# Own terms moved ahead of the update, and two PSUM banks shared by column, in layer 1 of a four-layer graph network

## The chip, the cores and the metric

One core of one Trainium2 chip runs the whole network in one launch. The metric is the device time of that launch in microseconds (us). Engines are named as the profile names them: PE (TensorE matmul), PEld (its weight loads), DVE (VectorE), ACT (ScalarE), POOL (GpSimd) and SP (SyncE, which here only issues DMAs).

## The reference

N = 2708 nodes have 128 features each; the adjacency matrix has about 0.6% entries that are not zero. Four layers follow one another, each with a residual and a layer norm. The change lies in layer 1, which is, cut to what matters:

```
s = x @ msg_w[:, :D].T                  # own term of each node
d = x @ msg_w[:, D:].T                  # a neighbour's term
messages   = gelu(s[:, None] + d[None, :] + msg_b)
aggregated = einsum('ijd,ij->id', messages, adj)
new = concat([x, aggregated]) @ upd_w.T + upd_b
h   = gelu(new) + x ;  h = layernorm(h) * ln_w + ln_b
x   = layernorm(x + h)
```

Layer 2, `A @ (x @ W) + b`, is partly done beside it.

## The kernel before

The rows are sorted by the number of their neighbours and cut into 22 blocks of up to 128. Layer 1 goes through the blocks in 22 turns, in the order `TURNS`. `CAPS` gives the neighbours of a block's longest row, 30 in the first and 8 in the shortest.

A turn has these parts.

- `own_row` (L854) loads the block's own rows by a DMA of SP into `x_s`: half 0 holds d of the node itself, half 1 holds x. The pool has three buffers. The loop asks for it one turn ahead.
- `messages` (L865) takes a PSUM bank `po` (tile `own`, one buffer). In its first quarter it transposes x (L870); ACT copies that into `x_st` (L871); two matmuls put the own term, with the bias, into the second quarter `s_ps` (L872, L873). DVE adds it to the node's own d (L887), ACT applies Gelu (L888), DVE weighs it (L882). For each chunk of up to 8 neighbours POOL issues one gather per neighbour slot (L247, an indirect DMA into `msg`, five buffers), DVE adds `s_ps` (L896), ACT applies Gelu (L899), and DVE weighs and accumulates each slot (L884) in the first and last quarters of `po`; the last two go to `parts` in SBUF. In turns 3 to 9 and 15 to 19 two `spread` calls follow, which lay out lists for layer 3: DVE multiplies (L618), PE multiplies into the third quarter of `po` (L624), DVE copies out (L631, L632).
- For the later blocks of the adjacency, `transposed` (PE L964, L969 and ACT L974 copies, SP writes L976) and `extract` (DVE, the neighbour lists) are emitted next.
- `update` (L905) takes the PSUM bank `tail` (one buffer). PE transposes and sums the two parts (L910), ACT copies (L917), PE multiplies with the two weights and the bias (L919 to L921), ACT applies Gelu (L926), DVE adds and normalises twice (L927 to L935), POOL scatters the new rows (L936, helper line L255), PE transposes them (L937) and multiplies with layer 2's weight (L941), with ACT copies L939 and L942. `x_b` (L915) is a sum that the first layer norm adds; it has two buffers.
- Further `transposed` calls for the earlier blocks, and from turn 11 on two `layer2` calls a turn (two at most; POOL gathers a row of the transposed adjacency, ACT writes `weighed` in L1007, one buffer, PE does L1014 and L1018).

No order is written out by hand here. A scheduler puts each engine's instructions into one fixed queue at compile time: among those that it takes to be ready, the one that stands earlier in the program goes first. It also derives all semaphores from what the instructions read and write. On the chip each queue runs strictly in its order.

Of the kernel before, what the change touches and what calls it, by code (L numbers as in the profile page):

```python
# [9 lines left out]
FP = mybir.dt.float32  # L10
AF = mybir.ActivationFunctionType
ALU = mybir.AluOpType
# [3 lines left out]
P = 128  # L16
N = 2708
D = 128
NFULL = N // P
NREM = N - NFULL * P  # L20
NBLK = NFULL + 1
# [40 lines left out]
BLOCKS = [(b * P, min(P, N - b * P)) for b in range(NBLK)]  # L62
# [5 lines left out]
TURNS = [*range(19), 21, 19, 20]  # L68
# [17 lines left out]
def gnn_resnorm_kernel(  # L86
# [21 lines left out]
    nc = tc.nc  # L108

    const = ctx.enter_context(tc.tile_pool(name="const", bufs=1))  # L110
    ident = const.tile([P, P], FP, name="ident")
# [127 lines left out]
    ones = keep.tile([P, P], FP, name="ones")  # L239
# [92 lines left out]
    own_ps = graph.enter_context(tc.tile_pool(name="own_ps", bufs=1, space=PSUM))  # L332
# [4 lines left out]
    with ExitStack() as layer:  # L337
# [355 lines left out]
        ws_t = weight(msg_w[:, 0:D], "ws_t")  # L693
# [3 lines left out]
        msgb = row_on_all(work, msg_b, "msgb")  # L697
# [151 lines left out]
        mine = layer.enter_context(tc.tile_pool(name="mine", bufs=2))  # L849
        bank = graph.enter_context(tc.tile_pool(name="bank", bufs=6, space=PSUM))  # L850
        tail_ps = graph.enter_context(tc.tile_pool(name="tail_ps", bufs=1, space=PSUM))
        xw = xs

        def own_row(b):  # L854
            n = BLOCKS[b][1]
            x_s = mine.tile([P, 2, D], FP, name="x_s", bufs=3)
            nc.sync.dma_start(
                x_s[0:n],
                dx_dram[int(b >= SPLIT)][b * P : b * P + n, 0 : 2 * D].rearrange(
                    "p (t d) -> p t d", t=2  # L860
                ),
            )
            return x_s

        def messages(b, x_s, three):  # L865
            n, kk = BLOCKS[b][1], CAPS[b]
            po = own_ps.tile([P, 512], FP, name="own", tag="own")
            x_st, s_ps = mine.tile([P, P], FP, name="x_st"), po[:, P : 2 * P]
            acc = (po[:, 0:P], po[:, 3 * P : 4 * P])
            nc.tensor.transpose(po[:, 0:n], x_s[0:n, 1, :], ident[0:n, 0:n])  # L870
            nc.scalar.copy(x_st[:, 0:n], po[:, 0:n])  # L871
            nc.tensor.matmul(s_ps[0:n], lhsT=x_st[:, 0:n], rhs=ws_t, start=True, stop=False)  # L872
            nc.tensor.matmul(  # L873
                s_ps[0:n], lhsT=ones[0:1, 0:n], rhs=msgb[0:1, :], start=False, stop=True
            )
            parts = mine.tile([P, 2, D], FP, name="parts")
            def weigh(k, m):
                last = acc[k % 2][0:n]
                to = parts[0:n, k % 2, :] if k >= kk - 1 else last
                v = ls[0:n, b, k : k + 1]  # L880
                if k < 2:
                    nc.vector.tensor_scalar(to, m, v, None, ALU.mult)  # L882
                else:
                    nc.vector.scalar_tensor_tensor(to, m, v, last, ALU.mult, ALU.add)  # L884

            mk = x_s[0:n, 0, :]
            nc.vector.tensor_tensor(mk, mk, s_ps[0:n], ALU.add)  # L887
            nc.scalar.activation(mk, mk, AF.Gelu)  # L888
            weigh(0, mk)
            for c0, c1 in chunks_of(kk):  # L890
                kc = c1 - c0
                msg = msgs.tile([P, 8, D], FP, name="msg")
                for k in range(kc):
                    gather(msg[0:n, k, :], d_dram, idx[0:n, b, c0 + k + 1 : c0 + k + 2])
                mk = msg[0:n, 0:kc, :]
                nc.vector.tensor_tensor(  # L896
                    mk, mk, s_ps[0:n].unsqueeze(1).to_broadcast((n, kc, D)), ALU.add
                )
                nc.scalar.activation(mk, mk, AF.Gelu)  # L899
                for k in range(kc):  # L900
                    weigh(c0 + k + 1, msg[0:n, k, :])
            for i, b3 in enumerate(three):
                spread(b3, po, 256 + 64 * i)
            return x_st, parts

        def update(b, x_s, x_st, parts):
            n = BLOCKS[b][1]
            tp = tail_ps.tile([P, 512], FP, name="tail")
            for i in range(2):
                nc.tensor.matmul(  # L910
                    tp[:, 0:n], lhsT=parts[0:n, i, :], rhs=ident[0:n, 0:n],
                    start=(i == 0), stop=(i == 1),
                )
            x_b = mine.tile([P, D], FP, name="x_b")
            nc.vector.tensor_tensor(x_b[0:n], x_s[0:n, 1, :], lnb[0:n], ALU.add)  # L915
            agg_t = mine.tile([P, P], FP, name="agg_t")
            nc.scalar.copy(agg_t[:, 0:n], tp[:, 0:n])  # L917
            pn = tp[0:n, P : 2 * P]
            nc.tensor.matmul(pn, lhsT=x_st[:, 0:n], rhs=u1_t, start=True, stop=False)  # L919
            nc.tensor.matmul(pn, lhsT=ones[0:1, 0:n], rhs=updb[0:1, :], start=False, stop=False)  # L920
            nc.tensor.matmul(pn, lhsT=agg_t[:, 0:n], rhs=u2_t, start=False, stop=True)  # L921
            new = mine.tile([P, 1, D], FP, name="new")
            x_n = mine.tile([P, 1, D], FP, name="x_n")
            sums = mine.tile([P, 2], FP, name="sums1")
            h, s0, s1 = new[0:n, 0, :], sums[0:n, 0:1], sums[0:n, 1:2]
            nc.scalar.activation(h, pn, AF.Gelu)  # L926
            nc.vector.scalar_tensor_tensor(  # L927
                h, h, 1.0, x_s[0:n, 1, :], ALU.mult, ALU.add, accum_out=s0
            )
            rstd = deviation(mine, n, 1, new[0:n], s0)  # L930
            nc.vector.scalar_tensor_tensor(h, h, s0, lnw[0:n], ALU.add, ALU.mult)
            nc.vector.scalar_tensor_tensor(
                h, h, rstd[0:n, 0:1], x_b[0:n], ALU.mult, ALU.add, accum_out=s1
            )
            normalised(mine, n, 1, new[0:n], s1, x_n[0:n])  # L935
            scatter(x2_dram, perm[0:n, b : b + 1], x_n[0:n, 0, :])  # L936
            nc.tensor.transpose(tp[:, 256 : 256 + n], x_n[0:n, 0, :], ident[0:n, 0:n])  # L937
            x_nt = mine.tile([P, P], FP, name="x_nt")
            nc.scalar.copy(x_nt[:, 0:n], tp[:, 256 : 256 + n])  # L939
            px = tp[0:n, 384:512]  # L940
            nc.tensor.matmul(px, lhsT=x_nt[:, 0:n], rhs=w2_l2, start=True, stop=True)  # L941
            nc.scalar.copy(xw[0:n, b, :], px)  # L942

# [86 lines left out]

        rows_of[NFULL] = searched_again(NFULL)
        again = list(range(SPLIT))
        ahead = own_row(0)
        left = list(range(SPLIT, NBLK))
        for i, b in enumerate(TURNS):
            if i == SPLIT - 2:
                sorted_lists(1)
            x_s, ahead = ahead, own_row(TURNS[i + 1]) if i + 1 < NBLK else None
            three = beside3(i)
            if i == 2 or i == SPLIT + 1:  # L1040
                for b3 in beside3(i + 1):
                    load3(b3)
            for b3 in beside3(i + 2) if three or beside3(i + 1) else []:
                load3(b3)
            x_st, agg = messages(b, x_s, three)
            for _ in range(2 if i < 1 else 1):
                if left:
                    e = left.pop(0)
                    with behind():
                        transposed(e, rows_of[e], True)  # L1050
                        run(extract(e, rows_of[e]))
                    if e == NBLK - 3:
                        run(place(SPLIT, NBLK - 2, lists(SPLIT, NBLK - 2)))
                    if e == NBLK - 1:
                        run(place(NBLK - 2, NBLK, lists(NBLK - 2, NBLK)))
            update(b, x_s, x_st, agg)
            if second and i:
                own_scatter(*second.pop(0))
            if i == 2:
                column_sums_of(0)  # L1060
            if i == 10:
                column_sums_of(1)

            for _ in range(2 if i in (9, 10, 11) else 1):
                if i and again:
                    e = again.pop(0)
                    transposed(e, load(e))
            if i == 11:
                accs2.extend(banks("acc2_"))
            if i >= 11:  # L1070
                for k in range(2 * (i - 11), min(i, 2 * (i - 10))):
                    layer2(k)
# [25 lines left out]
    with ExitStack() as layer:  # L1098
# [26 lines left out]
        for b0, count, n in quads():  # L1125
# [5 lines left out]
            for j in range(count):  # L1131
                nc.tensor.matmul(
                    ps_v[:, 0:D], lhsT=ones[0:n, :], rhs=sq[0:n, j, :],
                    start=(b0 + j == 0), stop=(b0 + j == NBLK - 1),
# [48 lines left out]
        for b0, count, n in quads():  # L1183
# [34 lines left out]
            for j in range(count):  # L1218
                at = slice(j * P, j * P + n)
# [19 lines left out]
    with ExitStack() as layer:  # L1239
        work = layer.enter_context(tc.tile_pool(name="s3", bufs=1))  # L1240
        mine = layer.enter_context(tc.tile_pool(name="s3_mine", bufs=2))
# [55 lines left out]
        own, closing, finishing, preparing, wide, sums_of = {}, [], [], [], [], {}  # L1297
# [242 lines left out]
        ahead = repeated(*quads[0], gathered[0])  # L1540
# [556 lines left out]
```

## Time and profile before

| | us |
|---|---|
| median of 3 runs (1930.33 to 1936.26) | 1935.91 |
| the profiled execution's own time | 1938.44 |
| its span, first to last instruction | 1936.7 |
| layer 1's turns, first transpose L870 to the last copy L942 | 204.5 to 1025.8 |

Busy time in that stretch of 821.3 us, from the view of busy time in windows: PE 388.4, PEld 318.6, DVE 380.3, ACT 239.3, POOL 406.9. The granted clock of TensorE is 0.61 of full speed in it, the DMA engines are busy 0.46.

A row of a group or tile view reads: line, engine, operation, out<-in, count, then durations (least, median, greatest, in ns) and first and last start. A row of the timeline reads: start, duration, engine, line, operation, out<-in, shapes, count, and in brackets the engine's idle time before it and what ended it; "remote" is a semaphore whose last update the view can't put to an instruction.

### The profile page before, as it was taken

How to read it: one execution, taken by the hardware profiler on the slowest of the kernel's cores; microseconds unless marked ns; L12 is line 12 of the kernel's file. 1: busy time of each engine (PE TensorE's matmuls, PEld its weight loads, DVE VectorE, ACT ScalarE, POOL GpSimd, SP SyncE). 2: the span in 40 equal slices, each digit the busy share in tenths (PEclk: the TensorE clock that was granted, in tenths of full speed). 3: DMA queues.
4: the chain of work that ended last, by engine and by line, in shares of the span. 5: the costliest groups of instructions: out<-in, count | busy, mean ns of one | idle time of the engine just before them, and what ended most of it. 6: DMA issues, size and time to landing. Idle time of an engine off the chain costs nothing. (4 is left out here: it accounts for less than half of the span.)

```text
span 1936.7 us, 23643 instructions
## 1 busy us (share of the span) xinstructions
PE 1240.9 (64%) x5771; PEld 864.1 (45%) x5771; DVE 1166.6 (60%) x4895; ACT 776.5 (40%) x3156; POOL 892.8 (46%) x1003
## 2 busy tenths in 40 slices
PE   7974313353446553554673748888788788878885
PEld 7973212242334442554663314544444444444444
DVE  8997445675635423433447417777678677676774
ACT  3565345543324210211122415555455555445553
POOL 1004654445653366445331474655555556555430
PEclk9986555555555576776676756676676777666675
DMA  8642645666545525223231574865566655756540
GB/s 283 238 150 79 131 140 165 174 183 174 141 103 142 177 43 160 95 92 140 79 113 44 167 239 131 212 190 163 145 196 183 182 166 160 191 150 192 150 115 7
DMA packets 167676, 289.63 MB, mean 150 GB/s; under 512 B 49600, under 2 KB 121502, under 8 KB 160429
## 3 DMA queue, kind: packets, MB, share of 16 engines
q0 software_dynamic: 60496, 190.77, 34.4%
q1 hardware_dynamic: 99489, 92.57, 15.6%
q10 hardware_dynamic: 7544, 4.69, 1.0%
q8 instruction: 48, 0.79, 0.2%
q14 instruction: 99, 0.81, 0.1%
HBM read 242.51 MB, written 45.36 MB: 149 GB/s over the span
## 5 line engine op out<-in xcount | busy, mean ns | idle before, releaser
L247 POOL DMA_INDIRECT g<-t_dram,idx x400 | 398.6, 996 | 316.0 <-issue 178.9
L247 POOL DMA_INDIRECT msg<-d_dram,idx x368 | 348.6, 947 | 260.2 <-issue 164.8
L1389 ACT ACTIVATE sum_junk<-g 126x128 bf16<-126x128 f32 (+3 forms) x1024 | 301.3, 296 | 142.4 <-issue 59.8
L1358 PE MATMUL z<-x,copies 32*126 32x512 f32 (+3 forms) x800 | 221.3, 944 | 65.8 <-DVE g L1555 45.0
L969 PE MATMUL pt_a<-ident,rows 128*128 128x128 f32 (+2 forms) x475 | 114.1, 395 | 144.4 <-ACT at_sb L974 79.5
L1555 DVE TENSOR_TENSOR g<-g,z 126x1536 f32<-126x1536 f32 (+3 forms) x100 | 175.0, 1750 | 44.0 <-DMA g<-t_dram,idx 15.3
L1018 PE MATMUL acc<-x_nat,at_rows 128*128 128x128 f32 (+2 forms) x968 | 160.7, 326 | 52.3 <-DMA at_rows<-at_dram,perm 26.5
L1389 ACT ACTIVATION_READ_ACCUMULATOR sum_junk<-g 126x1 f32 (+3 forms) x1024 | 191.6, 187 | 0.0
L1018 PEld LDWEIGHTS acc<-x_nat,at_rows 128*128 128x128 f32 (+2 forms) x968 | 144.1, 232 | 65.5 <-issue 38.7
L1363 PE MATMUL z<-g,ident 126*126 126x512 f32 (+3 forms) x200 | 169.3, 941 | 0.7 <-issue 0.7
L1435 PE MATMUL po_s<-wm,g 126*128 126x24 f32 (+6 forms) x800 | 128.6, 316 | 58.5 <-DVE wm L1422 56.2
L1435 PEld LDWEIGHTS po_s<-wm,g 126*128 126x128 f32 (+3 forms) x800 | 124.8, 243 | 75.6 <-DVE wm L1422 67.9
L969 PEld LDWEIGHTS pt_a<-ident,rows 128*128 128x128 f32 (+2 forms) x475 | 82.9, 205 | 167.5 <-ACT at_sb L974 92.8
L884 DVE SCALAR_TENSOR_TENSOR own<-msg,ls,own 128x128 f32<-128x128 f32 (+1 forms) x302 | 105.6, 350 | 85.4 <-ACT msg L899 28.5
L1381 DVE SCALAR_TENSOR_TENSOR g<-g,a_ps 126x1536 f32<-126x1536 f32 (+6 forms) x100 | 151.0, 1510 | 0.0
L420 PE MATMUL acc<-x_nat,rows 128*128 128x129 f32 (+3 forms) x1012 | 128.5, 288 | 26.0 <-DMA rows<-in_adj_dram 14.9
L420 PEld LDWEIGHTS acc<-x_nat,rows 128*128 128x128 f32 (+2 forms) x1012 | 123.0, 198 | 31.2 <-DMA rows<-in_adj_dram 16.0
L1358 PEld LDWEIGHTS z<-x,copies 32*126 32x126 f32 (+3 forms) x800 | 67.8, 261 | 100.3 <-issue 46.5
L899 ACT ACTIVATE msg<-msg 128x896 f32<-128x896 f32 (+4 forms) x55 | 50.4, 917 | 132.9 <-DVE msg L896 92.1
L1373 DVE SCALAR_TENSOR_TENSOR g<-z,a 126x128 f32<-126x128 f32 (+3 forms) x400 | 91.9, 285 | 19.5 <-remote 9.2
L445 DVE FIND_INDEX8 ci<-cv,rows 128x8 uint32<-128x247 f32 (+2 forms) x242 | 98.7, 408 | 0.0
L1363 PEld LDWEIGHTS z<-g,ident 126*126 126x126 f32 (+3 forms) x200 | 42.0, 263 | 124.3 <-issue 117.3
(302 smaller groups left out, 2132.2 us busy)
## 6 DMA issues: line engine op xcount, KB each, us to landing
rows<-in_adj_dram SPq DMA_DIRECT2D x34, 1354.0 KB
at_dram<-at_sb SPq DMA_DIRECT2D x105, 256.0 KB
g<-t_dram,idx POOLq DMA_INDIRECT x400
msg<-d_dram,idx POOLq DMA_INDIRECT x368
t_dram<-t_row SPq DMA_DIRECT2D x21, 256.0 KB
x_s<-dx_dram SPq DMA_DIRECT2D x21, 128.0 KB
at_dram<-at_sb SPq DMA_DIRECT2D x21, 64.0 KB
t_dram<-x_nat SPq DMA_DIRECT2D x5, 256.0 KB
```

The lines of the kernel that those rows point to most:

```text
L247: nc.gpsimd.indirect_dma_start(out=dst, out_offset=None, in_=table[0:N, :], in_offset=bass.IndirectOffsetOnAxis(ap=index, axis=0),)
L420: nc.tensor.matmul(accs0[k][0:m, c0 : c0 + f1 - f0], lhsT=rows[0:n, j0 : j0 + m], rhs=x_nat[0:n, b, f0:f1], start=k not in started, stop=( ...
L445: nc.vector.max_index(out=ci[0:n, at], in_max=cv[0:n, at], in_values=rows[0:n, c0 : c0 + cw])
L884: nc.vector.scalar_tensor_tensor(to, m, v, last, ALU.mult, ALU.add)
L969: nc.tensor.transpose(pt[0:m, j, 0:n], rows[0:n, c0 : c0 + m], ident[0:n, 0:n])
L1018: nc.tensor.matmul(accs2[ib // 4][0:m, (ib % 4) * D : (ib % 4 + 1) * D], lhsT=at[0:n, i0 : i0 + m], rhs=xw[0:n, b, :], start=(k == 0 and i ...
L1358: nc.tensor.matmul(z3[0:e, r, :] if r < 3 else z1[0:e], lhsT=copies[g][rows, j, :], rhs=own[b][1][rows, :], start=True, stop=r < 3, skip_g ...
L1363: nc.tensor.matmul(z1[0:e], lhsT=ident[0:e, 0:e], rhs=g4[0:e, 3, 0:HD], start=False, stop=True, skip_group_check=True,)
L1381: nc.vector.scalar_tensor_tensor(z, z, 0.0, a_ps[0:e].unsqueeze(1).to_broadcast((e, count, HD)), ALU.max, ALU.mult)
L1389: nc.scalar.activation(junk[0:e], g4[0:e, r, hd * D : (hd + 1) * D], AF.Identity, accum_out=sc[0:e, r, hd : hd + 1],)
L1435: nc.tensor.matmul(po[:, p0 * HEADS : (p0 + g) * HEADS], lhsT=g4s[i][0:e, r, HD : HD + D], rhs=wm[0:e, 4 * i + r, :, :], start=True, stop= ...
L1555: nc.vector.tensor_tensor(z, z, z3[0:e], ALU.add)
```

## The change

The own term is computed in a function of its own, `own_terms`, which the loop calls for the next turn's block after this turn's `messages` and `transposed`/`extract` and before this turn's `update`. Its transpose and its two matmuls use the second quarter of a bank `sums1` that is taken once for all turns. A new ACT copy moves the own term from PSUM to an SBUF tile `s` (two buffers), and the two adds of `messages` read `s`. The accumulators and the spreads use the other quarters of `sums1`. `own_row` is asked for two turns ahead. The updates get a bank `updates`, also taken once, of which even turns use the first half and odd turns the second; the last transpose and product use the columns that the first ones used. `x_b` has one buffer.

```diff
+        def own_terms(b, x_s):
+            n = BLOCKS[b][1]
+            x_st = mine.tile([P, P], FP, name="x_st")
+            s = mine.tile([P, D], FP, name="s")
+            at = sums1[:, P : 2 * P]
+            nc.tensor.transpose(at[:, 0:n], x_s[0:n, 1, :], ident[0:n, 0:n])
+            nc.scalar.copy(x_st[:, 0:n], at[:, 0:n])
+            nc.tensor.matmul(at[0:n], lhsT=x_st[:, 0:n], rhs=ws_t, start=True, stop=False)
+            nc.tensor.matmul(at[0:n], lhsT=ones[0:1, 0:n], rhs=msgb[0:1, :], start=False, stop=True)
+            nc.scalar.copy(s[0:n], at[0:n])
+            return x_s, x_st, s
...
-        def messages(b, x_s, three):
+        def messages(b, x_s, s, three):
...
-            po = own_ps.tile([P, 512], FP, name="own", tag="own")
-            x_st, s_ps = mine.tile([P, P], FP, name="x_st"), po[:, P : 2 * P]
-            acc = (po[:, 0:P], po[:, 3 * P : 4 * P])
-            nc.tensor.transpose(po[:, 0:n], x_s[0:n, 1, :], ident[0:n, 0:n])
-            nc.scalar.copy(x_st[:, 0:n], po[:, 0:n])
-            nc.tensor.matmul(s_ps[0:n], lhsT=x_st[:, 0:n], rhs=ws_t, start=True, stop=False)
-            nc.tensor.matmul(
-                s_ps[0:n], lhsT=ones[0:1, 0:n], rhs=msgb[0:1, :], start=False, stop=True
-            )
+            acc = (sums1[:, 0:P], sums1[:, 3 * P : 4 * P])
...
-            nc.vector.tensor_tensor(mk, mk, s_ps[0:n], ALU.add)
+            nc.vector.tensor_tensor(mk, mk, s[0:n], ALU.add)
...
-                    mk, mk, s_ps[0:n].unsqueeze(1).to_broadcast((n, kc, D)), ALU.add
+                    mk, mk, s[0:n].unsqueeze(1).to_broadcast((n, kc, D)), ALU.add
...
-                spread(b3, po, 256 + 64 * i)
-            return x_st, parts
+                spread(b3, sums1, 256 + 64 * i)
+            return parts
...
-        def update(b, x_s, x_st, parts):
+        def update(b, x_s, x_st, parts, tp):
...
-            tp = tail_ps.tile([P, 512], FP, name="tail")
...
-            x_b = mine.tile([P, D], FP, name="x_b")
+            x_b = mine.tile([P, D], FP, name="x_b", bufs=1)
...
-            nc.tensor.transpose(tp[:, 256 : 256 + n], x_n[0:n, 0, :], ident[0:n, 0:n])
+            nc.tensor.transpose(tp[:, 0:n], x_n[0:n, 0, :], ident[0:n, 0:n])
...
-            px = tp[0:n, 384:512]
+            px = tp[0:n, P : 2 * P]
...
-        ahead = own_row(0)
+        sums1 = own_ps.tile([P, 512], FP, name="sums1", tag="own")
+        updates = tail_ps.tile([P, 512], FP, name="updates", tag="tail")
+        rows1 = [own_row(b) for b in TURNS[:2]]
+        terms = [own_terms(TURNS[0], rows1.pop(0))]
...
-            x_s, ahead = ahead, own_row(TURNS[i + 1]) if i + 1 < NBLK else None
+            x_s, x_st, s = terms.pop(0)
+            if i + 2 < NBLK:
+                rows1.append(own_row(TURNS[i + 2]))
...
-            x_st, agg = messages(b, x_s, three)
+            agg = messages(b, x_s, s, three)
...
-            update(b, x_s, x_st, agg)
+            if rows1:
+                terms.append(own_terms(TURNS[i + 1], rows1.pop(0)))
+            update(b, x_s, x_st, agg, updates[:, 256 * (i % 2) : 256 * (i % 2) + 256])
```

More of the change, by code (lines that the diff above doesn't have):

```diff
@@ L936, in update @@
             scatter(x2_dram, perm[0:n, b : b + 1], x_n[0:n, 0, :])
-            nc.tensor.transpose(tp[:, 256 : 256 + n], x_n[0:n, 0, :], ident[0:n, 0:n])
+            nc.tensor.transpose(tp[:, 0:n], x_n[0:n, 0, :], ident[0:n, 0:n])
             x_nt = mine.tile([P, P], FP, name="x_nt")
-            nc.scalar.copy(x_nt[:, 0:n], tp[:, 256 : 256 + n])
-            px = tp[0:n, 384:512]
+            nc.scalar.copy(x_nt[:, 0:n], tp[:, 0:n])
+            px = tp[0:n, P : 2 * P]
             nc.tensor.matmul(px, lhsT=x_nt[:, 0:n], rhs=w2_l2, start=True, stop=True)
```

## The prediction

> **What bounds the kernel now.** I read the page first. Its chain of waits ends at the last output DMA and tells nothing of layer 1. The slices show no engine full between 204.5 and 1025.8 us, where the turns of layer 1 lie, so this stage is bound by waits. I then read the timeline of each turn by the lines 870, 871, 873, 887, 884, 632 and 910. A turn starts when the bank `own` is free again, and the next one can't start before. Turn 2 shows how it begins, in the PE and then the DVE timeline:
>
> ```profile
> 348.36 1.23 PE L910 MATMUL tail<-ident,parts 128*128 128x128 f32 x4 [12.27 <-DVE parts L884]
> 349.38 0.42 PE L870 MATMUL own<-ident,x_s 128*128 128x128 f32 x1
> ...
> 349.94 0.80 PE L919 MATMUL tail<-u_t,x_st 128*128 128x128 f32 x2
> 350.67 0.79 PE L920 MATMUL tail<-updb,ones 1*128 1x128 f32 x2
> 351.39 0.80 PE L921 MATMUL tail<-u_t,agg_t 128*128 128x128 f32 x2
> 351.98 0.63 PE L872 MATMUL own<-ws_t,x_st 128*128 128x128 f32 x2
> 352.54 0.79 PE L873 MATMUL own<-msgb,ones 1*128 1x128 f32 x2
> ```
> ```profile
> 353.44 0.29 DVE L887 TENSOR_TENSOR x_s<-x_s,own 128x128 f32<-128x128 f32 x1 [0.91 <-PE own L873]
> ```
>
> The reader is to see that the next block's own term already starts 1.4 us after the last `parts` (348.0 us), beside turn 1's update, with no change made. PE only does four matmuls of L910 ahead of L870 and the six of L919 to L921 ahead of L872, and DVE then waits for L873.
>
> Summed over the 22 turns, from start and end times in the timeline: from the release of the bank to L870 56.6 us, L870 to L871 68.9, L871 to the end of L873 48.8, from there to L887 32.6; the messages from L887 to the last `parts` take 466.8, the spreads 134.1. The first four, 207 us, are what the change is about.
>
> **Is the own term really ahead?** Only if PE may write one quarter of the bank while DVE adds up in the others. The rows of the tile `spread` answer that:
>
> ```profile
> L624 PE MATMUL own<-of_chunk,spread x96: 176/368/404, 417.9 to 967.9; 128*126 128x16 f32 x20, 128*128 128x16 f32 x20, 128*126 128x20 f32 x16, 128*126 128x12 f32 x16
> L618 DVE TENSOR_TENSOR spread<-lists,of_row x48: 271/283/354, 336.4 to 967.1; 128x126 f32<-128x126 f32 x26, 128x128 f32<-128x128 f32 x14, 128x125 f32<-128x125 f32 x4, 128x120 f32<-128x120 f32 x4
> ```
>
> The first spread was ready at 336.4, its matmul uses columns that no accumulator touches, and yet it ran at 417.9, 0.7 us after turn 3's last `parts` began. In all 12 turns with spreads L624 first comes after the last `parts`. So the order is kept by bank. The new transpose writes the same bank and stands behind `messages` and its spreads in the program: it can't start earlier than L870 does now. What is left is a change of precedence and one more copy.
>
> **The change part by part.**
>
> *Added copy.* 22 ACT copies of 128x128 out of PSUM, at the 265 ns of L871, on the path from L873 to the add, with a plain hand-over of 0.05 us (from L871 to L872 in turn 5, 471.50 to 471.55): 22 x 0.315 = +7 us.
>
> *Added hand-over.* The add now waits for ACT, which waits for PE. Hand-overs are at times far longer than plain, while POOL issues its gathers back to back; turn 5 is such a case (ACT):
>
> ```profile
> 471.07 0.28 ACT L926 ACTIVATE new<-tail 128x128 f32<-128x128 f32 x1 [21.27 <-remote]
> 471.24 0.26 ACT L871 COPY x_st<-own 128x128 f32<-128x128 f32 x1
> ```
>
> The matmul that L926 waits for ends at 452.1 by its record; POOL issues until 469.3. The price of one more hand-over is bounded by nothing and by the 32.6 us between L873 and L887; without turn 1, which has 19.4 of them, it is 13.2. I take +13, since 17 of the 22 are under 0.3 us.
>
> *ACT held.* ACT now waits in its queue for L873, which today only DVE does. From L871's end to L873's end pass about 1.6 us; ACT is busy 173 of 436 us in the first ten turns and 66 of 385 in the last twelve, so 10 x 1.6 x 0.40 + 12 x 1.6 x 0.17 = 10 us of work (`at_sb` copies, Gelu) is pushed back. Ends: 0 and 22 x 1.6 = 35. I take +10. Queued behind are L974, for which SP's writes wait.
>
> *Precedence.* `own_terms` now stands ahead of `update`. At the 9 turn changes without spreads L870 need not pass L910: 349.38 - 348.36 = 1.02 us each, -9. In turns 1, 2, 3, 11 and 14 L871 to the end of L873 takes 3.5 us and not 1.9, since L919 to L921 or their like lie between: -8. With spreads L910 is ready long before and nothing changes. The update is pushed back by the same 1.5 to 2 us; it runs beside the messages, which hide it except in the last turn, where no own term follows.
>
> *The adds from SBUF.* L915 adds two SBUF tiles in 281 ns, L887 takes 287 with one in PSUM: 0. The Trainium skill, "SBUF — State Buffer", section "Who interferes with whom", says that a Vector instruction with two SBUF inputs contends with a GpSimd instruction that reads SBUF, and that the loser stands still for the whole instruction. By that rule each of the 77 adds could wait out an issue of 0.94 us, 72 us as an estimate. The row of L618, two SBUF inputs, is 271/283/354 ns with POOL at work beside many: 77 x 0.07 = 5 us at most, and I keep 0.
>
> *Rows two turns ahead.* The three buffers of `x_s` are filled at 200.5, 200.9 and 203.7 today, and the fourth load goes at 315.9, just after turn 0's L927 has read its buffer (315.6). SP issues as early as the buffers allow already: 0. SP waits for L927 124 us in all in the stretch of the turns, as before.
>
> *Halves of one bank, one buffer of `x_b`.* L910 waited for L942 once, for 0.2 us; `x_b` is read by DVE (L932) before the next L915, on the same engine. Both 0, hidden by the messages.
>
> Sum: 7 + 13 + 10 - 9 - 8 = +13 us. The profiled execution took 1938.4, 2.5 above the median shown; 1935.9 + 13 = **1949 us** for the median.
>
> **The rivals.**
>
> *Own terms escape from blocked queues (faster).* In five turns L871 stands behind something in ACT's queue and L870 to L871 takes 12.5 (turn 5), 17.9 (14), 9.0 (16), 9.6 (18) and 10.4 us (19), where 0.5 is usual. Turn 14, ACT:
>
> ```profile
> 763.72 0.40 ACT L1007 ACTIVATE weighed<-ones,column_sum 128x128 f32<-128x128 f32 x1 [16.58 <-remote]
> 778.42 0.40 ACT L1007 ACTIVATE weighed<-ones,column_sum 128x128 f32<-128x128 f32 x1 [14.30 <-issue]
> 783.33 0.27 ACT L917 COPY agg_t<-tail 128x128 f32<-128x128 f32 x1 [4.50 <-remote]
> 783.49 0.27 ACT L871 COPY x_st<-own 128x128 f32<-128x128 f32 x1
> ```
>
> If L871 gets ahead of L1007 in turns 14 and 19, 17.4 + 9.9 = 27 us go: -27 - 17 + 20 = -24, 1912 us. It decides if L871 precedes L1007 there and the copy of `s` brings no new block. For it: the own term is ready 1 to 2 us sooner, and all queues are laid out anew. Against it: these two are the seventh and eighth of L1007, which the loop emits at the end of turn 14, behind turn 14's own term already; the scheduler drew them ahead because it took them to be ready first, and the program's order did not help.
>
> *Nothing reaches the end (within 0.3%).* The messages, 467 us, contain waits of ACT for the adds (92 us) and stretches where POOL issues back to back; a delay of under 1 us a turn may vanish there, and the gains cancel the copy (7 against 17): -5 to +5, 1931 to 1941.
>
> *The change does what it says.* If PE may fill the quarter while DVE adds in the others, most of the 207 us goes; with two thirds of it, 138, the time is 1798. The rows of L624 speak against it in 12 of 12 turns.
>
> **How the numbers follow.** Forecast (slower): 0.50, 1942 to 1980, the upper part with both unknown costs near their ends (7 + 33 + 35 - 17 = +58 would be 1994). Escape, or another luckier layout of the queues: 0.28. Nothing: 0.20. Really ahead: 0.02. The queues are laid out anew by the scheduler, so that each turn's blocks may fall otherwise; this spreads each case by some 10 us. About 0.3%, 5.8 us, is what a measurement of this kernel can tell from no change. Faster 0.30, same 0.20, slower 0.50. For 8 in 10 the range takes in the escape at 1912 with a little below it, and most of the forecast's own range: 1907 to 1976. The forecast's own range is 1942 to 1980.
>
> **What would show it.** Right: the first own transpose of a turn still follows the last weighing and the spreads; the new copy comes 22 times at about 265 ns; ACT idles before it for PE; the first add waits for ACT and not PE. The precedence is right if the own transpose stands ahead of the four matmuls on `parts` where no spread lies between. Wrong: an own transpose amid a turn's weighings (then the bank is not the unit, and the time falls by tens of us); `weighed` waits before `x_st` gone (the escape); adds longer than 1.3 us beside gathers (the port); SP standing longer at the loads of `x_s`.

## The result, and the profile after

The changed kernel takes 1958.05 us (median of 8 runs, 1945.37 to 1964.21). The kernel before, run beside it, takes 1929.51 us (8 runs, 1926.08 to 1936.26). The ratio on record is 1.0129, with a 95% interval of 1.0104 to 1.0154: slower by about 25 us (the two medians lie 28.5 apart). The profiled execution took 1951.33 us, its span is 1949.6. Ratios leave out runs that lie over 1.5% above the fastest of the same kernel: in the experiments below one of e7's, four of e9's and one of the kernel before in the third group.

| layer 1's turns, us | before | after |
|---|---|---|
| first own transpose to last `xw` copy | 204.5 to 1025.8: 821 | 204.6 to 1045.8: 841 |
| busy DVE / ACT | 380 / 239 | 374 / 243 |
| busy PE / POOL | 388 / 407 | 403 / 416 |
| release of the bank to the own transpose, summed over 22 turns | 56.6 | 35.7 |
| own transpose to the copy `x_st` | 68.9 | 76.6 |
| copy `x_st` to the end of the own matmuls | 48.8 | 56.3 |
| own matmuls to the first add | 32.6 | 60.7 |
| first add to the last `parts` | 466.8 | 471.2 |
| spreads | 134.1 | 126.8 |

The new lines are 871 (own transpose), 872 (`x_st`), 873 and 874 (own matmuls), 875 (the added copy), 892 (first add), 914 (`parts` into the update's bank), 946 (`xw`, which the trace calls `x_nat`).

PE's timeline at a turn change, the one that the prediction showed of before:

```profile
318.96 0.80 PE L945 MATMUL updates<-w_l,x_nt 128*128 128x128 f32 x2 [1.27 <-DMA at_dram<-at_sb]
319.55 0.42 PE L871 MATMUL sums<-ident,x_s 128*128 128x128 f32 x1
320.12 1.23 PE L914 MATMUL updates<-ident,parts 128*128 128x128 f32 x4
322.72 0.80 PE L873 MATMUL sums<-ws_t,x_st 128*128 128x128 f32 x2 [1.38 <-issue]
323.45 0.79 PE L874 MATMUL sums<-msgb,ones 1*128 1x128 f32 x2
```

L871 now stands ahead of L914, and no L923 to L925 stand between L914 and L873. Both orders are as the diff asks. Here L914 begins only at 320.12, just after the last copy L946 of the update before it (ACT, 319.80 to 320.07).

The rows of the bank `sums` and of the tile `spread`, which carry the question whether the own term is really ahead:

```profile
L624 PE MATMUL sums<-of_chunk,spread x96: 177/263/402, 398.5 to 978.1; 128*126 128x16 f32 x20, 128*128 128x16 f32 x20, 128*126 128x20 f32 x16, 128*126 128x12 f32 x16
...
L871 PE MATMUL sums<-ident,x_s x22: 272/421/477, 204.6 to 1006.5; 128*128 128x128 f32 x21, 20*128 20x20 f32 x1
```
```profile
L618 DVE TENSOR_TENSOR spread<-lists,of_row x48: 271/283/364, 384.8 to 974.3; 128x126 f32<-128x126 f32 x26, 128x128 f32<-128x128 f32 x14, 128x125 f32<-128x125 f32 x4, 128x120 f32<-128x120 f32 x4
```

A spread is ready at 384.8 and its matmul runs at 398.5; in all 21 turn changes L871 comes after the turn's last write of the accumulators or the last read of the spreads (0.1 us after it in the least case). This fits an order that is kept by bank, and the own term isn't ahead.

The groups of the touched instructions after (busy, mean ns of one, then the idle time before them and what ended it):

```profile
L255 POOL DMA_INDIRECT x_dram<-x_n,perm x22 | 22.9, 1042 | 135.2 <-DVE x_n L321 72.3 <-DVE sums L889 47.9 <-DVE sums L887 11.5
...
L892 DVE TENSOR_TENSOR x_s<-x_s,s 128x128 f32<-128x128 f32 (+1 forms) x22 | 6.5, 293 | 94.0 <-ACT s L875 50.4 <-issue 40.9 <-ACT x_nat L946 2.7
...
L875 ACT COPY s<-sums 128x128 f32<-128x128 f32 (+1 forms) x22 | 5.8, 265 | 50.2 <-remote 31.5 <-PE sums L874 14.5 <-PE pt_a L973 2.6
...
L872 ACT COPY x_st<-sums 128x128 f32<-128x128 f32 (+1 forms) x22 | 5.8, 262 | 88.8 <-remote 44.3 <-PE sums L871 36.5 <-PE pt_a L973 2.5
```

The added copy comes 22 times at 265 ns, ACT idles for PE before it, and DVE's first add waits for ACT 50.4 us, as forecast. The first line was not in the forecast: it is the scatter that ends each update (helper line 255), and POOL stands 135 us at it, 133 before. It is read again below.

Read as a chain from turn to turn, the table above accounts for the 20 us: the start got 22 longer (-21 +8 +8 +28), the messages 4, the spreads 7 shorter. The experiments show that this account is not a cause.

### The profile page after: what moved, and what is told of

Same layout as the page of the kernel before. It is cut to its first block, busy times and chain, and to the rows that moved or that the text cites. A ratio compares the mean times of both kernels' runs of the same rounds, so it can differ in the third digit from the quotient of the medians.

```text
span 1949.6 us, 23677 instructions
## 1 busy us (share of the span) xinstructions
PE 1249.4 (64%) x5771; PEld 871.6 (45%) x5771; DVE 1160.0 (59%) x4895; ACT 778.7 (40%) x3178; POOL 903.9 (46%) x1003
## 5 line engine op out<-in xcount | busy, mean ns | idle before, releaser
L247 POOL DMA_INDIRECT msg<-d_dram,idx x368 | 354.8, 964 | 226.1 <-issue 172.4
L1369 PE MATMUL z<-x,copies 32*126 32x512 f32 (+3 forms) x800 | 211.4, 916 | 59.5 <-DVE g L1566 36.0
L1022 PE MATMUL acc<-x_nat,at_rows 128*128 128x128 f32 (+2 forms) x968 | 175.9, 335 | 57.6 <-issue 57.3
L1022 PEld LDWEIGHTS acc<-x_nat,at_rows 128*128 128x128 f32 (+2 forms) x968 | 152.7, 237 | 75.2 <-issue 72.3
L1446 PE MATMUL po_s<-wm,g 126*128 126x24 f32 (+6 forms) x800 | 135.5, 326 | 61.5 <-DVE wm L1433 57.8
L1446 PEld LDWEIGHTS po_s<-wm,g 126*128 126x128 f32 (+3 forms) x800 | 131.4, 255 | 78.5 <-DVE wm L1433 68.9
L889 DVE SCALAR_TENSOR_TENSOR sums<-msg,ls,sums 128x128 f32<-128x128 f32 (+1 forms) x302 | 105.5, 349 | 102.4 <-ACT msg L904 46.1
L1369 PEld LDWEIGHTS z<-x,copies 32*126 32x126 f32 (+3 forms) x800 | 62.5, 252 | 92.3 <-issue 47.7
L450 DVE MAX8 cv<-rows 128x8 f32<-128x247 f32 (+2 forms) x242 | 95.5, 400 | 2.4 <-POOL rows L410 2.4
```

What stands on the lines that cost most here:

```text
L247: nc.gpsimd.indirect_dma_start(out=dst, out_offset=None, in_=table[0:N, :], in_offset=bass.IndirectOffsetOnAxis(ap=index, axis=0),)
L1022: nc.tensor.matmul(accs2[ib // 4][0:m, (ib % 4) * D : (ib % 4 + 1) * D], lhsT=at[0:n, i0 : i0 + m], rhs=xw[0:n, b, :], start=(k == 0 and i ...
L1369: nc.tensor.matmul(z3[0:e, r, :] if r < 3 else z1[0:e], lhsT=copies[g][rows, j, :], rhs=own[b][1][rows, :], start=True, stop=r < 3, skip_g ...
L1446: nc.tensor.matmul(po[:, p0 * HEADS : (p0 + g) * HEADS], lhsT=g4s[i][0:e, r, HD : HD + D], rhs=wm[0:e, 4 * i + r, :, :], start=True, stop= ...
```

## The experiments

Kernels of one group ran on one chip, beside the kernel before; each ratio is to that. "Ahead" means own terms emitted ahead of the update, as in the change; "behind" means at the start of the turn that uses them.

**First group: the parts of the change** (before: 1930.73 us, 25 runs).

*e1*, the kernel before with the copy alone (and one buffer of `x_b`):

```
+            s = mine.tile([P, D], FP, name="s")
+            nc.scalar.copy(s[0:n], s_ps[0:n])
...
-            nc.vector.tensor_tensor(mk, mk, s_ps[0:n], ALU.add)
+            nc.vector.tensor_tensor(mk, mk, s[0:n], ALU.add)
```

> The kernel before with one thing added: ACT copies the own term from PSUM to an SBUF tile s, and both adds read s; x_b gets one buffer to make room. Place and order in the program stay as before. Theory 1 (the copy and its hand-over cost, ACT is held by it): +20 to +35 us against before, with the time from the own matmuls' end to the first add growing from 33 to about 55 us in 22 turns. Theory 2 (the loss comes from own terms standing ahead of the update, which pushes the updates back): within 0.3%, 0 to +6 us. Theory 3 (any new layout of the queues costs or gains by chance): -10 to +10 us.

Measured: 1940.86 us, ratio 1.0054 (1.0022 to 1.0086). The loss of 10 us lies between the first two theories, at the end of the third's range, and its interval lies above 1.

*e2*, the change without the copy (the adds read the quarter of `sums1` in PSUM):

```
-            nc.scalar.copy(s[0:n], at[0:n])
-            return x_s, x_st, s
+            return x_s, x_st, at
```

> The changed kernel without the copy: the own term stays in its quarter of the bank and the adds read it there; it is still computed ahead of the update. Theory 1: faster than before by what precedence gains, -10 to -20 us, since the copy is gone. Theory 2: the loss stays, +15 to +30 us. Theory 3: -10 to +10 us.

Measured: 1948.68 us, ratio 1.0119 (1.0063 to 1.0176), from 4 runs. Taking the copy out gives nothing back that these runs can show.

*e3*, the change with own terms behind the update:

```
-            x_s, x_st, s = terms.pop(0)
+            x_s, x_st, s = own_terms(b, rows1.pop(0))
...
-            if rows1:
-                terms.append(own_terms(TURNS[i + 1], rows1.pop(0)))
```

> The changed kernel with the call of the own terms moved to the start of the turn that uses them, behind the last turn's update, as before; the copy, the two banks and the rows two turns ahead stay. Theory 1: the precedence gain is lost too, so +30 to +45 us against before, slower than the changed kernel. Theory 2: the updates start early again, 0 to +10 us against before, and no update waits for the last copy of the one before. Theory 3: no relation to either, -10 to +30.

Measured: 1929.76 us, ratio 0.9992 (0.9962 to 1.0021). The copy, the halves of one bank, the single `x_b` and the rows two ahead are all still there: the order alone carries the loss.

*e4*, the own term in the third quarter of the updates' bank and emitted ahead of the messages:

```
-            at = sums1[:, P : 2 * P]
+            at = updates[:, 2 * P : 3 * P]
...
+            if i + 1 < NBLK:
+                terms.append(own_terms(TURNS[i + 1], rows1.pop(0)))
             agg = messages(b, x_s, s, three)
...
-            update(b, x_s, x_st, agg, updates[:, 256 * (i % 2) : 256 * (i % 2) + 256])
+            update(b, x_s, x_st, agg, updates[:, 0:256])
```

> The changed kernel with the own term's quarter taken from the updates' bank (third quarter; both updates use the first half) and the own terms of the next block emitted ahead of this turn's messages. PE can then fill it while DVE adds up in the other bank. If the start of a turn sets the pace (all three theories so far), the four parts from the bank's release to the first add, 207 us before and 229 after, shrink to under 60, and the time falls by 100 us or more, below 1850. The rival: gathers, late releases or PE and ACT queues set the pace of a turn instead, and the messages grow by what the start gives up: -40 to +10 us.

Measured: 1937.79 us, ratio 1.0047 (1.0025 to 1.0068), as the rival expected. Here the own term really is a turn ahead. PE's timeline in e4, turn 1's own transpose while turn 0's messages run until 273.9:

```profile
211.27 0.47 PE L871 MATMUL updates<-ident,x_s 128*128 128x128 f32 x1 [3.79 <-issue]
...
214.13 0.80 PE L873 MATMUL updates<-ws_t,x_st 128*128 128x128 f32 x2 [0.46 <-issue]
214.85 0.79 PE L874 MATMUL updates<-msgb,ones 1*128 1x128 f32 x2
```

The start of the turn is off the chain, yet the messages grow to 578 us, and the six parts of the turns sum to 811 us (808 before, 827 in the change). The profiled e3 shows the reverse: its four start parts are longer than before (78, 107, 77 and 80 us, 342 in sum), its messages take 323, and all six 801. Start and messages trade against each other, so neither by itself sets the pace of these kernels.

**Second group: two candidates for the cause** (before: 1918.51 us, 19 runs).

*e5* and *e6*, the change and the kernel before with the scatter emitted behind the next turn's messages:

```
-            scatter(x2_dram, perm[0:n, b : b + 1], x_n[0:n, 0, :])
+            rows2.append((perm[0:n, b : b + 1], x_n[0:n, 0, :]))
...
+            if rows2:
+                scatter(x2_dram, *rows2.pop(0))
```

> The changed kernel, with one thing moved: the scatter of a block's new rows is emitted behind the next turn's messages, so that POOL need not stand at it before the next gathers. In the changed kernel POOL issues for 537 us of the stretch of the turns (416 busy, 121 of short gaps) and stands still for about 300, of which 132 at 11 of these scatters. Theory of the closed loop (POOL's gathers, messages, update, scatter, POOL again sets the pace, so that an update pushed back holds the next gathers): a good part of the 132 goes, 1958 falls to 1860..1930. Rival (POOL would then wait at the message buffers instead, the pace is set elsewhere): 1950..1965 with the idle time of POOL moved to the gathers.

> The kernel before, with the same move of the scatter alone. POOL stands 130 us at 12 of the 22 scatters there. Closed loop: 1830..1915, faster than before. Rival (idle time only moves to the message buffers): 1920..1940.

Measured: 1940.60 us, ratio 1.0147 (1.0083 to 1.0210, 4 runs), and 1920.84 us, 1.0018 (0.9983 to 1.0053). Inconclusive: the scheduler had already put each scatter that far back, and every queue came out instruction for instruction as without the edit. As repeats on another chip they have a use: the change gives 1.0147 again, and the kernel before measured against itself gives 1.0018.

*e7*, the change with the last transpose and product of each update emitted behind the next turn's update:

```
+            products.append(update(b, x_s, x_st, agg, updates[:, 256 * (i % 2) : 256 * (i % 2) + 256]))
+            if i:
+                product(*products.pop(0))
```

It tests a wait that the trace after shows, on PE where turn 10's update begins:

```profile
695.06 1.22 PE L914 MATMUL updates<-ident,parts 128*128 128x128 f32 x4 [4.81 <-ACT x_nat L946]
696.08 0.42 PE L871 MATMUL sums<-ident,x_s 128*128 128x128 f32 x1
```

The `parts` of turn 10 had been ready since 665.5. L914 begins 0.05 us after the previous update's last copy (L946); both use halves of one bank. L871, behind it in PE's queue, is the own transpose of turn 12; the last `parts` of turn 11, for which it had to wait, were ready at 681.4. In 9 turns of the changed kernel a late L914 begins within 0.5 us of the end of L946.

> The changed kernel, with the last transpose, its copy, the product and its copy of each update emitted behind the next turn's update; nothing else moves. In the changed kernel the first matmul of 8 of 22 updates begins right behind the previous update's last copy, since both use one bank. Theory (this wait is what the halves of one bank cost once own terms stand ahead of the update): the wait goes and 1958 falls by 10..25 to 1933..1948. Rival (the late copy only shows that ACT's queue stood still for another reason, and the update would be late without it): 1950..1965.

Measured: 1923.56 us, ratio 1.0025 (0.9991 to 1.0059). It fits the theory, but e3's trace speaks against it: there L914 starts even later after the last `parts` (198 us summed over 22 turns; 163 in the change, 50 before, 24 in e7), behind a last copy in 12 turns, and e3 costs nothing. e9 and e10 below were the controls.

*e8*, the network left out: a chain of hand-overs beside gathers.

> The network is left out. A chain of 5 x 40 cycles, each a PE transpose, an ACT copy and a DVE multiplication of 128x128 that wait for each other: phase 1 alone, 2 beside 120 row gathers of POOL, 3 alone, 4 beside 120 plain DMAs of SP of the same size, 5 beside 120 POOL copies. Theory (while POOL issues gathers back to back, the other engines' semaphores are released late, as their update times in the trace of before suggest): a cycle takes about 1.2 to 1.6 us in phases 1, 3, 4 and 5, and at least 4 us in phase 2. Rival (the lateness is the DMA traffic's, or belongs to that kernel's queues): phase 2 like phase 1, or phase 4 as slow as phase 2.

Measured from the starts of the transposes: 1.09 us a cycle in phase 1; 1.25 beside the first 31 gathers, then 2.1 to 2.9; 1.09 (median) in phases 3, 4 and 5, with a few cycles of up to 2.1 in phases 3 and 4. The effect is there, at half the size expected.

**Third group: the factors crossed** (before: 1917.34 us, 28 runs). *e9* is e3 with e7's late product; *e10* is e7 without the copy; *e11* is e9 without the copy.

> The changed kernel, with own terms behind the update again and the last transpose and product of each update behind the next turn's update: the two edits that each brought the time back (0.999 and 1.003 of before) together. Theory (both take away the same wait, that of an update for the previous update's last copy, which own terms ahead of the update brought): no further gain, 0.995..1.004 of before, about 1922..1940 where before is 1931. Rival (the late product is a gain by itself that hid a remaining loss): 0.985..0.994.

> The changed kernel without the copy of the own term (the adds read PSUM) and with the late product. Without the copy but with the wait the ratio was 1.012. Theory (the wait of the updates for the previous update's last copy is the cost of the order): 0.996..1.004. Rival (own terms ahead of the update cost by themselves, by holding PE and ACT from the update): 1.007..1.015.

> The changed kernel with own terms behind the update, the late product, and no copy of the own term: what is left of the change are rows two turns ahead, halves of one bank, one buffer of x_b. Theory of the prediction (the copy and its hand-over cost some 10 us and the rest nothing): 0.990..0.998 of before. Rival (the copy costs nothing where the accumulation waits for it anyway): 0.998..1.005.

| own terms | copy | product | ratio to before (95%) |
|---|---|---|---|
| ahead | yes | as changed | 1.0129 (1.0104 to 1.0154), the change |
| ahead | no | as changed | 1.0119 (1.0063 to 1.0176), e2 |
| ahead | yes | late | 1.0025 (0.9991 to 1.0059), e7 |
| ahead | no | late | 1.0080 (1.0051 to 1.0108), e10 |
| behind | yes | as changed | 0.9992 (0.9962 to 1.0021), e3 |
| behind | no | as changed | 1 by definition, the kernel before (it has full banks and rows one ahead) |
| behind | yes | late | 0.9975 (0.9935 to 1.0015), e9 |
| behind | no | late | 1.0022 (0.9990 to 1.0054), e11 |

e9 and e11 fell where no further gain and no cost of the copy were expected (the theory of e9, the rival of e11). e10 fell in its rival's range, and this speaks against the wait that e7 removed: in e10 L914 starts only 20 us after the last `parts`, summed over 22 turns, and 0.8% is lost all the same.

Read in pairs. **Ahead minus behind**: +0.0137, +0.0119, +0.0050, +0.0058, the same sign four times, in the mean +0.009, about 17 us. In the last two pairs, those with the late product, the intervals overlap, and the third rests on which of e9's runs count: with all runs the medians of e7 and e9 are 1.0026 and 1.0007 of before's, a difference of +0.002. So the first two pairs show that the order costs; the last two only agree in sign. **Copy minus none**: +0.0010, -0.0055, -0.0008, -0.0047, and +0.0054 in e1: no common sign, though e1's own interval is clear of 1. **Late product**: -0.0104 and -0.0039 with own terms ahead, -0.0017 and +0.0022 behind: it gives back part of what the order costs and is no gain by itself. No version beats the kernel before measurably.

*e12*, the network left out: the hand-overs by engine.

> The network is left out. Four phases, each 90 cycles beside 100 row gathers of POOL and then 8 cycles alone: PE, ACT and DVE in turn; DVE and ACT; PE and ACT; PE and DVE. In the first such run a cycle of PE, ACT and DVE took 1.09 us alone, 1.25 us beside the first 31 gathers and 2.1 to 2.9 beside the next, the whole excess between the end of the transpose and the start of ACT's copy. Theory (what comes late is PE's release): cycles of DVE and ACT stay below 1.3 us, those with PE reach 2 us or more after some 30 gathers whether ACT or DVE waits for it. Rival (what stands still is ACT's, which shares the path to POOL's descriptors): DVE and ACT slow down as well, PE and DVE don't.

Measured, median time from the end of one instruction to the start of the next:

| hand-over | cycles alone | beside the later gathers |
|---|---|---|
| PE to ACT or DVE | 0.04 us | 1.75 to 2.00 us |
| ACT to DVE, in the chain of these two | 0.03 us | 0.84 us |
| ACT to DVE, in the chain of all three | 0.03 us | 0.03 us |
| DVE to ACT | 0.03 us | 0.03 us |
| DVE or ACT to PE | 0.06 us | 0.06 us |

Neither theory was whole: PE's release is late whether ACT or DVE waits for it; ACT's is late as well, and less, in the chain without PE, but not in the chains with PE; DVE's not at all. The timeline of e12, all engines, first beside the early gathers and then beside the later ones:

```profile
32.10 0.48 PE L61 MATMUL pt<-ident,chain 128*128 128x128 f32 x1 [0.78 <-issue]
32.30 0.95 POOL L98 DMA_INDIRECT got<-in_x_dram,idx_all  x1 [0.30 <-issue]
32.62 0.27 ACT L63 COPY mid<-pt 128x128 f32<-128x128 f32 x1 [0.99 <-issue]
32.91 0.38 DVE L65 TENSOR_SCALAR chain<-mid 128x128 f32<-128x128 f32 x1 [0.87 <-issue]
...
62.95 0.47 PE L61 MATMUL pt<-ident,chain 128*128 128x128 f32 x1 [2.33 <-issue]
...
64.77 0.94 POOL L98 DMA_INDIRECT got<-in_x_dram,idx_all  x1 [0.30 <-issue]
65.17 0.27 ACT L63 COPY mid<-pt 128x128 f32<-128x128 f32 x1 [2.53 <-remote]
65.46 0.30 DVE L65 TENSOR_SCALAR chain<-mid 128x128 f32<-128x128 f32 x1 [2.57 <-issue]
```

The transpose ends at 32.58 and ACT starts at 32.62; the later one ends at 63.42 and ACT starts at 65.17, called "remote". In the chain of DVE and ACT (their two timelines put together) ACT's copy ends at 255.04 and DVE starts at 255.87, while DVE's end at 254.70 releases ACT at once:

```profile
254.47 0.23 DVE L72 TENSOR_SCALAR chain<-mid 128x128 f32<-128x128 f32 x1 [1.15 <-ACT mid L70]
254.74 0.30 ACT L70 COPY mid<-chain 128x128 f32<-128x128 f32 x1 [1.08 <-issue]
255.87 0.23 DVE L72 TENSOR_SCALAR chain<-mid 128x128 f32<-128x128 f32 x1 [1.17 <-issue]
```

**What the order does.** In each of these kernels POOL issues some 428 instructions in the turns, for 527 to 537 us with the 0.30 us between them (407 us busy before and 416 after, and some 121 us of such gaps). For the rest of the stretch, which is 810 to 841 us long, POOL stands, mostly at two things: gathers that need a free `msg` buffer, and the scatter of an update's rows (rows and table below count the 0.30 us as idle too). The row of that scatter, in three kernels with own terms behind (before, e3, e11) and then in e10, ahead:

```profile
L255 POOL DMA_INDIRECT x_dram<-x_n,perm x22 | 21.9, 993 | 132.8 <-DVE x_n L321 67.1 <-DVE own L884 47.5 <-DVE spread L618 15.1
```
```profile
L255 POOL DMA_INDIRECT x_dram<-x_n,perm x22 | 22.5, 1023 | 96.6 <-DVE x_n L321 40.6 <-DVE sums L889 31.1 <-DVE spread L618 9.2
```
```profile
L255 POOL DMA_INDIRECT x_dram<-x_n,perm x22 | 21.7, 987 | 120.1 <-DVE sums L887 66.8 <-DVE x_n L321 30.7 <-DVE spread L618 19.6
```
```profile
L255 POOL DMA_INDIRECT x_dram<-x_n,perm x22 | 21.7, 988 | 148.3 <-DVE sums L887 76.3 <-DVE x_n L321 58.8 <-DVE sums L885 10.2
```

| pair, ahead against behind | idle at the scatters, us | idle at the gathers, us | gathers of later turns that stand ahead of the 22 scatters in POOL's queue, sum |
|---|---|---|---|
| the change, e3 | 135.2, 96.6 | 226.1, 235.6 | 651, 702 |
| e2, before | 151.4, 132.8 | 230.4, 260.2 | 608, 662 |
| e7, e9 | 126.0, 105.6 | 226.6, 251.6 | 627, 663 |
| e10, e11 | 148.3, 120.1 | 249.3, 249.0 | 599, 648 |

In four pairs of four, with own terms ahead, POOL stands 19 to 39 us longer at the scatters, and 36 to 54 fewer gathers stand ahead of them in its queue, about two a turn. Nothing in the edit touches POOL. The scheduler, which lays out all queues at once, puts each scatter earlier among the gathers of the following turns, and what was queued behind now waits for it. In turns 13 to 18 of the change each scatter stands at most five gathers behind the next turn's last one; the longest case in POOL's timeline:

```profile
914.98 0.94 POOL L247 DMA_INDIRECT at_rows<-at_dram,perm  x1 [0.30 <-issue]
942.89 1.85 POOL L255 DMA_INDIRECT x_dram<-x_n,perm  x1 [26.97 <-DVE sums L889]
```

POOL stands 27 us with gathers queued behind. In the kernel before, the scatters of turns 13 to 18 stand 5 to 15 gathers behind the next turn's last one, in e3 5 to 18.

That this costs the time is not shown. Part comes back at the gathers in three of the pairs. The net is near the difference of the turns in the profiled executions of the change and e3 (39 less 10 against 28 us) and of e10 and e11 (28 against 20). In the other two pairs POOL stands 19 and 20 us longer at the scatters, and yet the profiled execution with own terms ahead is the shorter one, 1931.08 against 1938.44 and 1914.80 against 1924.20. They may not stand for their kernels: e2's was the fastest of its runs (median 1948.68), and e7's lies below its median (1923.56), e9's above (1918.71).

Against the kernel before, the change stands only 2 us longer at these scatters (135.2 and 132.8), with 11 fewer gathers ahead of them, while its turns are 20 us longer; e1, slower by 0.5%, stands 104.3 us, less than before. What grew between before and the change is POOL's wait at another scatter, that of lists for layer 3 (+31 us), its wait at the gathers of `at_rows` (+12) and its busy time (+9); at the gathers of `msg` it stands 34 us less. The rows of that other scatter, before and after:

```profile
L255 POOL DMA_INDIRECT lists_dram<-lists,rank x22 | 21.4, 973 | 35.6 <-issue 11.8 <-DVE lists L557 10.7 <-DVE deg L720 5.8
```
```profile
L255 POOL DMA_INDIRECT lists_dram<-lists,rank x22 | 22.3, 1013 | 66.5 <-DVE rs_t L275 19.8 <-DVE rs_y L271 13.8 <-DVE lists L557 10.8
```

It goes with the copy and not with the order (59 to 67 us in the change, e1, e3, e4, e7 and e9, which have the copy; 36 to 48 in before, e2, e10 and e11), and e3 has it too (64.3) without a loss. POOL's busy and idle times add up to the length of the stretch whatever sets the pace, so such a sum names places and no cause.

What stays open: by which path the order costs, and whether the place of the scatters is the cause or goes along with another one. The edit meant to move them (e5) left them where they were, and no run ties them behind later gathers. Why the late product helps only with own terms ahead is open too: its scatters stand no later (627 against 651), and POOL still stands 126 us at them.

## Why the prediction was right and wrong

The forecast of 1949 lies within the range of the runs, in part by luck: its base of 1935.9 was 6.4 us above the 1929.5 that the kernel before takes in all 8 runs, and measured against these the loss was 25 us where +13 was forecast. The sign was right by terms that don't hold.

- **Own term not ahead, by bank**: right, in 21 of 21 turn changes. That the 207 us at the start of the turns are what the change is about was wrong: e4 takes them off the chain and loses 0.5%, e3 lengthens them by 135 us and loses nothing. The premise "A turn starts when the bank `own` is free again, and the next one can't start before", read as what sets the pace, failed first, and all terms were sized on it.
- **Added copy +7, hand-over +13, ACT held +10**: each shows in the trace about as described (265 ns; own matmuls to first add 28 us longer against 20), and no cost stands out over five pairs, -0.0055 to +0.0054; alone, in e1, the copy went with +0.0054. That it lies on a path that waits for POOL's gathers anyway would explain this; no run shows it.
- **Precedence -9 -8**: the queue changed as forecast at the first transpose (release to transpose 21 us shorter); L872 to the last own matmul got 8 longer and not shorter. The term has the wrong sign: about +17 us in the mean of four pairs, +26 between the change and e3. The gain failed with the premise about the start. Where the cost comes from is open. The late start of the update is not it: "it runs beside the messages, which hide it" agrees with e3, whose L914 starts later than the change's in sum (198 against 163 us) and which loses nothing, and e10 loses 0.8% with 20 us. The forecast looked at PE's and ACT's queues; that POOL's is laid out anew as well, with the update's scatter among the gathers, it did not price.
- **Adds from SBUF 0**: right. L892 takes 293 ns and at most 342 (row of the tile `x_s`: 273/293/342) where L887 took 287; the chunk adds take 1049 ns in the mean, 1043 before. The rule of the Trainium skill, "SBUF — State Buffer", section "Who interferes with whom", that such an instruction can stand still beside GpSimd, does not show in these rows: 9 of the 22 L892 run beside a POOL instruction, and none waits out an issue of 0.94 us. e8 shows something near it: its DVE multiplication, with one SBUF tensor, goes from 0.23 to 0.38 us beside the first 31 gathers, whose period of 1.25 us the whole cycle takes on.
- **Rows two ahead, one `x_b`**: no cost seen, as forecast; e3 contains both at 0.999. SP's waits for the loads of `x_s` are 241 us before, all releasers together (the 124 of the forecast are those for L927 alone), and 232 after.
- **Halves of one bank 0**: wrong in the trace, since L914 comes late behind L946 in 9 turns; right in the time as far as e3 shows, where the same costs nothing.
- **Escape from blocked queues**: gave nothing. `x_st` came later (76.6 against 68.9 us), and ACT's idle time ahead of L872 was 44.3 us "remote" and 36.5 for PE. In turn 14 the seventh and eighth L1011 (L1007 before) no longer stand ahead of it, only the sixth does, and yet it comes 14.5 us after its transpose, where it was 17.9 (ACT's timeline after):

```profile
772.33 0.40 ACT L1011 ACTIVATE weighed<-ones,column_sum 128x128 f32<-128x128 f32 x1 [2.61 <-PE updates L914]
785.66 0.27 ACT L872 COPY x_st<-sums 128x128 f32<-128x128 f32 x1 [12.92 <-remote]
```

  The layout of the queues did change, as this rival's price assumed, but no gain came of it; POOL's queue changed too, as read above.

## What to carry to other kernels

When a scheduler lays out fixed queues, ask of an edit not only what it issues but where it moves every instruction that has others behind it, such as a scatter or store at the end of a step in the queue that also issues the next step's loads: here one call emitted earlier changed the order on an engine that it doesn't use. A chain that is followed from turn to turn can account for a difference to the microsecond and still not be its cause: check it by an edit that takes one term away (e4 took away the start, and the time did not follow). Idle times that add up, on one engine's queue or along the turns, are no cause either: compare them with the kernel before too, and not only between variants. Where an edit has two parts, cross them; a single removal (e7) supported a theory that a crossed one (e10) took back.

## What the runs showed of the hardware

While POOL issues row gathers back to back (one in 1.25 us: 0.94 and 0.30 between), some semaphores of other engines are released late. In the kernel before, between 200 and 1030 us, take the time from an instruction's end to the next recorded update of its semaphore. It is 0.01 us in the median for PE, DVE and ACT where POOL is idle for 3 us on either side. Where POOL issues for over 70% of that time, it is 1.8 us in the median and 3.3 in the mean for PE (25 at most), 0.5 and 1.6 for DVE, 0.9 and 4.8 for ACT. These are upper bounds: a fifth to a third of the updates have no record (322 of PE's 402 have one, 1078 of DVE's 1453, 291 of ACT's 447), and then a later one is taken.

e8 and e12 show it without the kernel, from the starts of the waiting instructions: nothing of it beside the first 22 to 31 gathers (8 in e12's third phase, which begins 6 us after the second's last gather), then 1.75 to 2.0 us from PE to its reader and 0.84 from ACT to DVE where no PE takes part, and, in the median, none beside plain DMAs or POOL's copies. It also outlasts the gathers: in e12's first, third and fourth phases PE's release is still late 13, 22 and 15 us after POOL's last gather has ended, when the last packets have ended too (141.1, 454.8 and 626.9 against packets that end last at 129.3, 433.7 and 613.0). So it is not an issue that holds a release at that moment; it looks like something that piles up and drains, and what that is stays open. Waits of 10 to 25 us did not come up there, so the simple chain doesn't cover all of it. All of this is from profiled executions; whether an execution without the profiler has it is not shown. It fits the "remote" waits of the timeline: there the record of the releasing instruction has long ended.
